# Side work one slot later: VectorE's additions to PE's results, and in_proj's input loaded two blocks ahead

## The chip, the cores and the metric

The kernel runs on one core of a Trainium2 chip. The metric is the device time of one execution in microseconds (us); lower is better. Engines are named as in the profile: PE (TensorE), DVE (VectorE), ACT (ScalarE), POOL (GpSimd) and SP (SyncE, which here issues every DMA). [...]

## The reference

Four layers on a tensor of 4 images x 64 x 64 tokens x 96 channels, all in float32:

```python
x = x + L0(group_norm(x))            # selective scan block, 192 inner channels, on 64 x 64 tokens
x = x + irfft2(L1(rfft2(x)))         # the same kind of block, 384 inner channels, on 64 x 33 frequencies
t = tokens(x)
for layer in (2, 3):
    t = t + attention(layer_norm(t)) # linear attention: (q k^T) v without a softmax, 6 heads
    t = t + ffn(layer_norm(t))       # 96 -> 384 -> 96, operands rounded to 8-bit floats
```

A selective scan block (L0 and L1) does this:

```python
xin, z = split(x @ in_proj_w.T)
u = silu(depthwise_conv3x3(xin) + conv_b)
for k in range(4):                   # rows, columns, and both backwards
    dt, B, C = split(x_proj[k] @ u_k)
    delta = softplus(dt_projs[k] @ dt + bias)
    h_t = h_(t-1) * exp(delta_t * A) + delta_t * u_t * B_t     # 16 states for each channel
    y_k = sum over the states of h_t * C_t
y = layer_norm(sum of y_k + D * u) * silu(z)
return y @ out_proj_w.T
```

## The kernel before

The recurrence is the body of the kernel. Channels lie on the 128 partitions, in three chunks `c`, and tokens on the free axis, in segments of up to 512. There are six **phases**: two for L0 (two images each, 64 partitions per image) and four for L1 (one image each). A phase runs the four directions `k`, each cut into segments; L0 has 8 segments of 512 in a direction, L1 has 5, of 512, 512, 384, 384 and 320. A segment is cut into 12 **steps** (4 groups `q` of four states by 3 chunks `c`). That makes 2 x 384 + 4 x 240 = 1728 steps.

A step has four scan instructions on DVE (L643), two into `hx` and two into `hy`. POOL multiplies `hx` by C (`hcx`, L789) and makes the input of the `hy` scans (L636). DVE multiplies `hy` by C (`hcy`, L807). ACT makes the decays exp(delta A) (L618). PE transposes the input of the next step's `hx` scans (L613) and adds up `hcx` and `hcy` in PSUM (L665). The order on the engines is written out by hand in `scans`; no scheduler moves anything.

Everything else is **side work**: generators that issue a little and then `yield`. In each step the function `slot` is called three times: on DVE's list slot 1 lies after the two `hx` scans, slot 2 between the two `hy` scans, and slot 3, the late one, ahead of `hcy`. On PE's list slot 1 lies ahead of the two transpositions for the next step, slot 2 behind them, and slot 3 between the additions of `hcx` and of `hcy`. A slot adds a third of the phase's entry in `RATES` to a balance and resumes the side work once if the balance is at least one:

```python
prepare_more(kind)
due = min(due + st.z.ph.rate / 3, 3.0)
if due >= 1.0:
    due -= E.step(kind)
```

`E.step` first issues what the generator left with `E.defer` at its last turn, then resumes the generator up to its next `yield`. After `yield LATE` the generator is resumed in a slot 3 only; a refused slot costs no balance. All side work that uses PSUM shares one buffer of one bank (tag `ms`). What a phase has not finished is carried into the next; what is left after the last step is run off with no scans beside it (`E.finish`).

The side work of the phases (with Python's function names) is: `flip0`, `begin0(1)` and two `gate0`; `end0(0)`, `begin1(0)`, `begin1(1)`; `end0(1)`, `begin1(2)`, `begin1(3)`; then `end1(0)`, `end1(1)`, `end1(2)`, one in each of the last three phases. `begin0` for the first two images runs ahead of all phases (the head, up to about 224 us), and `end1(3)` behind them (the tail, from about 11650 us); in both, a `yield` only hands the turn on.

These places of the side work matter here:

- `visits` is in_proj: it loads a block of up to 8 rows of its input (`xi`, L189, 240 to 384 KB, issued on SP), and per block has two turns with PE matmuls (L176). Two buffers (tag `xin`) hold the input; at the beginning of a block the next one is loaded. 48 calls, 228 blocks in all.
- `gated` normalizes: matmuls with the matrix of means into `pm` (L414, three turns), then three DVE subtractions of `pm` from `yb` (L417).
- `out0`: out_proj of L0, two turns of 12 matmuls into `po` (L884), then one DVE addition (L893) and the store of its result.
- `tokens`, attention: four matmuls into `pao` (L1155), then a deferred DVE addition to the tokens (L1157), then the next group's transpositions (L1149).
- `tokens`, feed-forward: matmuls `pfo` (L1184), a deferred ACT copy to `y16` (L1192), then, after `yield LATE`, two DVE additions (L1194, L1198) and the next group's transpositions (L1164).

Of the kernel before, what the change touches and what calls it, by code (L numbers as in the profile page):

```python
# [6 lines left out]
F32 = mybir.dt.float32  # L7
# [10 lines left out]
NB, HH, WW, CH = 4, 64, 64, 96  # L18
# [4 lines left out]
SM = 512  # L23
LATE, BURST = "late", "burst"

RATES = [1.75, 2.25, 2.35, 2.35, 2.35, 2.35]
EXP_LN = "natural_log_exp_and_others"


# [94 lines left out]
class Block:  # L124
# [59 lines left out]
    def visits(self, E, sp, wi, xf, blocks, half, nm, w, done):  # L184


        def load(r, n):
            x = sp.tile([CH, 2, 512], F32, name=f"xi{half}_{nm}_{r}", tag=f"xin{w}", bufs=2)
            self.nc.sync.dma_start(out=x[:, :, : n * 64], in_=xf[:, :, r * 64 : (r + n) * 64])  # L189
            return x  # L190

        nxt = load(*blocks[0])
        yield
        yield
        for b, (r, n) in enumerate(blocks):
            x, nxt = nxt, load(*blocks[b + 1]) if b + 1 < len(blocks) else None
            pi = E.psum(f"pi{half}_{nm}_{r}")
            yield from self.in_proj(pi, wi, half, x, n * 64)
            E.defer(lambda r=r, n=n, pi=pi: done(r, n, pi))
            yield  # L200
# [149 lines left out]
    def gated(self, E, g, io, out_proj):  # L350


        nc, cfg = self.nc, self.cfg
        yn, yo = io["y"][cfg.nat], io["y"][1 - cfg.nat].rearrange("k (w r) c -> r w k c", r=cfg.NR)
        u, gz = io["u"][cfg.nat], io["gz"]
        with E.pool(f"{cfg.pre}nm{g}") as sp:
            wo = sp.tile([P, C, self.w["wo"].shape[2]], F32, name=f"{cfg.pre}_wo_{g}", tag="wo")
            nc.sync.dma_start(out=wo, in_=self.w["wo"])

            tiles = [  # L360
                (b, i, r + i, min(2, n - i)) for b, (r, n) in enumerate(cfg.rows) for i in range(0, n, 2)
            ]

            def load(b, i, r, n):
                nm = f"{cfg.pre}_{g}_{r}"
                yt = sp.tile([P, 2, 2, C * P], F32, name=f"yt_{nm}", tag="yt", bufs=2)
                nc.sync.dma_start(
                    out=yt[: n * 64, 0], in_=yn[:, r * 64 : (r + n) * 64, :].rearrange("k t c -> t k c")
                )
                for m in range(n):  # L370
                    nc.sync.dma_start(out=yt[m * 64 : (m + 1) * 64, 1], in_=yo[r + m])
                ut = sp.tile([P, C, P], F32, name=f"ut_{nm}", tag="ut", bufs=2)
                nc.sync.dma_start(out=ut[:, :, : n * 64], in_=u[:, :, r * 64 : (r + n) * 64])
                return yt, ut

            todo = iter(tiles)
            nxt = load(*next(todo))
            yield
            yield
            yield  # L380
            for b, (r, nr) in enumerate(cfg.rows):
                n = nr * 64
                nm = f"{cfg.pre}_{g}_{r}"
                z = sp.tile([P, C, 512], F32, name=f"zb_{nm}", tag="zb")
                nc.sync.dma_start(out=z[:, :, :n], in_=gz[:, :, r * 64 : r * 64 + n])
                y = sp.tile([P, C, 512], F32, name=f"yb_{nm}", tag="yb")
                for i in range(0, nr, 2):
                    m = min(2, nr - i) * 64
                    yt, ut = nxt
                    more = next(todo, None)  # L390
                    nxt = load(*more) if more else None
                    ps = E.psum(f"py_{nm}_{i}")[:, : C * P].rearrange("p (c t) -> p c t", c=C)
                    for c in range(C):
                        nc.tensor.matmul(
                            ps[:, c, :m], self.skip[:, c, :], ut[:, c, :m], start=(c == 0), stop=False
                        )
                    yield
                    for c in range(C):
                        for k in range(4):
                            nc.tensor.matmul(  # L400
                                ps[:, c, :m],
                                yt[:m, k // 2, k % 2, c * P : (c + 1) * P],
                                self.ident[:m, :m],
                                start=False,
                                stop=(c == C - 1 and k == 3),
                                is_transpose=True,
                            )
                        if c < C - 1:
                            yield
                    E.defer(lambda i=i, m=m, ps=ps, y=y: nc.scalar.copy(y[:, :, i * 64 : i * 64 + m], ps[:, :, :m]))  # L410
                    yield
                pm = E.psum(f"pm_{nm}")
                for c in range(C):
                    nc.tensor.matmul(pm[:, :n], self.mean_w, y[:, c, :n], start=(c == 0), stop=(c == C - 1))  # L414
                    yield
                for c in range(C):
                    nc.vector.tensor_tensor(y[:, c, :n], y[:, c, :n], pm[:, :n], ALU.subtract)  # L417
                yield
                sq = sp.tile([P, C, 512], F32, name=f"sq_{nm}", tag="sq")
                nc.scalar.activation(sq[:, :, :n], y[:, :, :n], AF.Square)  # L420
                yield
                pv = E.psum(f"pv_{nm}")
                for c in range(C):
                    nc.tensor.matmul(pv[:, :n], self.mean_w, sq[:, c, :n], start=(c == 0), stop=(c == C - 1))
                    yield
                ln = sp.tile([P, 512], F32, name=f"ln_{nm}", tag="ln")
                nc.scalar.activation(ln[:, :n], pv[:, :n], AF.Ln, bias=self.eps)
                nc.scalar.activation(pv[:, :n], ln[:, :n], AF.Exp, scale=-0.5)
                yield
                for c in range(C):  # L430
                    nc.vector.scalar_tensor_tensor(
                        y[:, c, :n], y[:, c, :n], self.lnw[:, c : c + 1], pv[:, :n], ALU.mult, ALU.mult
                    )
                yield LATE
                for c in range(C):
                    nc.vector.scalar_tensor_tensor(
                        y[:, c, :n], y[:, c, :n], self.lnb[:, c : c + 1], z[:, c, :n], ALU.add, ALU.mult
                    )
                yield
                yield from out_proj(E, sp, wo, y, r, nr)  # L440
# [429 lines left out]
def out0(images, ins, x0):  # L870


    def task(E, blk, sp, wo, y, r, nr):
        nc = E.nc
        PI = blk.cfg.PI
        tok = slice(r * 64, (r + nr) * 64)
        for i, b in enumerate(images):
            xr = sp.tile([P, 4, CH], F32, name=f"xr_{b}_{r}", tag="xr", bufs=2)
            nc.sync.dma_start(out=xr, in_=ins["x"][b, tok, :].rearrange("(t p) c -> p t c", p=P))
            po = E.psum(f"po_{b}_{r}")[:, : 4 * CH].rearrange("p (t c) -> p t c", t=4)  # L880
            half = slice(i * PI, (i + 1) * PI)
            for m in range(4):
                for c in range(C):
                    nc.tensor.matmul(  # L884
                        po[:, m, :],
                        y[half, c, m * P : (m + 1) * P],
                        wo[half, c, :],
                        start=(c == 0),
                        stop=(c == C - 1),
                    )  # L890
                if m % 2:
                    yield
            nc.vector.tensor_tensor(xr, xr, po, ALU.add)  # L893
            nc.sync.dma_start(out=x0[b][tok, :].rearrange("(t p) c -> p t c", p=P), in_=xr)

    return task
# [144 lines left out]
def tokens(E, ins, consts, ident, x1, b, out):  # L1041
# [4 lines left out]
    with E.pool(f"tk{b}") as sp:  # L1046
# [4 lines left out]
        x = sp.tile([P, NT, CH], F32, name=f"tok_{b}", tag="tok")  # L1051
# [52 lines left out]
        for ly in (2, 3):  # L1104
            nm = f"{b}_{ly}"
# [40 lines left out]
            for g in range(NT // 4):  # L1146
# [7 lines left out]
                for i in range(4):  # L1154
                    nc.tensor.matmul(po[:, i, :], xt[:, i * P : (i + 1) * P], wo, start=True, stop=True)  # L1155
                xs = x[:, g * 4 : g * 4 + 4, :]
                E.defer(lambda xs=xs, po=po: nc.vector.tensor_tensor(xs, xs, po, ALU.add))  # L1157
                yield

            yield from layer_norm(nm + "f")  # L1160
            for g in range(NT // 4):
# [28 lines left out]
                        )  # L1190
                y16 = sp.tile([P, 4, CH], F16, name=f"y16_{nm}_{g}", tag="y16")
                E.defer(lambda y16=y16, po=po: nc.scalar.copy(y16, po))  # L1192
                yield LATE
                nc.vector.tensor_tensor(  # L1194
                    y16, y16, q["b2"].rearrange("p (o c) -> p o c", o=1).to_broadcast([P, 4, CH]), ALU.add
# [206 lines left out]
```

## Time and profile before

| | |
|---|---|
| runs | 12104.8 us median of 3 (12100.4 to 12110.6) |
| profiled execution | 12108.8 us, of which the span of the trace is 12106.9 |
| busy, share of the span | DVE 87%, PE 78%, ACT 75%, POOL 74% |
| granted PE clock | 0.87 of full speed on average |
| scans run | from about 230 to 11650 us: 1728 steps in 11420 us, 6.6 us each |
| tail | 457 us |
| DMA | 44% of 16 engines' time, 120 GB/s |

The page gives busy time of each engine, the span in 40 slices (each digit is the busy share of a slice in tenths), groups of instructions, and who waited for whom. A line such as "DVE a L1 <- PE b L2: 50.0, 10, 9.0" says that DVE sat idle ahead of line 1, which writes a, until PE had done line 2, which writes b: 50.0 us in total, 10 times, 9.0 us at most. "L636 POOL" is line 636 of the kernel on POOL. The views can be cut to a stretch of time.

### The profile page before, as it was taken

To read this page: it belongs to the slowest core of one execution; us is meant where nothing else is said; L and a number is where in the kernel's file an instruction comes from. 1 tells how busy PE (TensorE), PEld (TensorE's weight loads), DVE (VectorE), ACT (ScalarE), POOL (GpSimd) and SP (SyncE) were. 2 spreads that over 40 slices of the span, in tenths; PEclk is the share of its full clock that TensorE was granted. 3 is DMA by queue.
4 is the path that set the end of the run, shared out by engine and by line. 5 is a ranking of instruction groups with operands and counts; after the bars stand their busy time and mean duration, and the time that the engine had idled before them with its cause. 6 is when DMAs were issued, how large, how long until landed. Compare 5 with 4: busy or idle time off the path is not lost. (4 is left out here: it accounts for less than half of the span.)

```text
span 12106.9 us, 164888 instructions
## 1 busy us (share of the span) xinstructions
PE 9441.0 (78%) x54800; PEld 6783.4 (56%) x54800; DVE 10572.7 (87%) x10183; ACT 9071.5 (75%) x18534; POOL 8900.0 (74%) x7074
## 2 busy tenths in 40 slices
PE   5677777777788778777888888788778877887765
PEld 2455555555666556556665565565556555565544
DVE  6899999999999999998879888988989899899854
ACT  3778888898778888887667777777777677777733
POOL 2888889888778888987668877877667766676630
PEclk8889999989889989998879889888878877898886
DMA  5554444556555445445543443444224422452231
GB/s 142 123 135 115 119 125 112 134 157 158 146 143 117 129 130 128 129 132 154 144 120 112 130 123 116 152 128 115 85 91 145 118 82 88 135 132 89 82 103 36
DMA packets 1270447, 1469.07 MB, mean 121 GB/s; under 512 B 496023, under 2 KB 1033823, under 8 KB 1260119
## 3 DMA queue, kind: packets, MB, share of 16 engines
q1 hardware_dynamic: 1269591, 1458.53, 44.1%
q8 instruction: 431, 7.06, 0.2%
q14 instruction: 425, 3.48, 0.1%
HBM read 1221.74 MB, written 236.50 MB: 120 GB/s over the span
## 5 line engine op out<-in xcount | busy, mean ns | idle before, releaser
L636 POOL TENSOR_TENSOR hy_l<-du_l,bc_l 128x512 f32<-128x512 f32 (+2 forms) x3456 | 3956.4, 1165 | 2266.6 <-DVE hcy_l L807 1206.7
L789 POOL TENSOR_TENSOR hcx_l<-hx_l,bc_l 128x1024 f32<-128x1024 f32 (+2 forms) x1616 | 3524.5, 2181 | 279.6 <-DVE hx_l L643 244.1
L593 ACT ACTIVATE bx_l<-dut_l,bt_l 128x192 f32<-128x192 f32 (+2 forms) x6272 | 2771.7, 498 | 0.1
L665 PE MATMUL acc_l<-ident,hcx_l 128*128 128x128 f32 (+1 forms) x12000 | 1885.7, 306 | 357.1 <-POOL hcx_l L789 353.3
L665 PE MATMUL acc_l<-ident,hcy_l 128*128 128x128 f32 (+1 forms) x11994 | 1850.5, 302 | 381.9 <-DVE hcy_l L807 378.5
L618 ACT ACTIVATE ax_l<-delta_l,l_alog 128x512 f32<-128x512 f32 (+2 forms) x3456 | 2139.3, 667 | 0.0
L665 PEld LDWEIGHTS acc_l<-ident,hcy_l 128*128 128x128 f32 (+1 forms) x11994 | 1550.1, 156 | 945.6 <-DVE hcy_l L807 571.3
L665 PEld LDWEIGHTS acc_l<-ident,hcx_l 128*128 128x128 f32 (+1 forms) x12000 | 1545.3, 157 | 852.5 <-POOL hcx_l L789 615.0
L807 DVE TENSOR_TENSOR hcy_l<-hy_l,bc_l 128x1024 f32<-128x1024 f32 (+2 forms) x1615 | 1950.7, 1208 | 43.0
L643 DVE TENSOR_TENSOR_SCAN hx_l<-ax_l,state_l,b_l 128x512 f32<-128x512 f32 (+2 forms) x1648 | 1786.8, 1125 | 222.8 <-PE b_l L613 142.1
L643 DVE TENSOR_TENSOR_SCAN hy_l<-b_l,state_l,hy_l 128x512 f32<-128x512 f32 (+2 forms) x1648 | 1789.7, 1121 | 143.8 <-ACT b_l L618 122.4
L618 ACT ACTIVATE b_l<-delta_l,l_alog 128x512 f32<-128x512 f32 (+2 forms) x1912 | 1200.4, 628 | 881.4 <-DVE hx_l L643 839.3
L613 PE MATMUL b_l<-ident,bx_l 128*128 128x128 f32 (+1 forms) x6718 | 1184.5, 303 | 408.3 <-DVE hy_l L643 193.5
L618 ACT ACTIVATE ab_l<-delta_l,l_alog 128x512 f32<-128x512 f32 x1321 | 909.3, 688 | 700.3 <-DVE hx_l L643 668.7
L613 PEld LDWEIGHTS b_l<-ident,bx_l 128*128 128x128 f32 (+1 forms) x6718 | 825.8, 152 | 905.8 <-DVE hy_l L643 296.7
L643 DVE TENSOR_TENSOR_SCAN hy_l<-ab_l,state_l,hy_l 128x512 f32<-128x512 f32 x961 | 1177.1, 1260 | 97.0 <-ACT ab_l L618 62.0
L643 DVE TENSOR_TENSOR_SCAN hx_l<-ax_l,state_l,ab_l 128x512 f32<-128x512 f32 x962 | 1177.5, 1265 | 95.6 <-PE ab_l L613 66.3
L613 PE MATMUL ab_l<-ident,bx_l 128*128 128x128 f32 x5288 | 903.3, 306 | 454.2 <-DVE hy_l L643 218.0
L656 POOL COPY state_l<-hx_l 128x2 f32<-128x2 f32 x1344 | 1114.3, 829 | 0.0
L613 PEld LDWEIGHTS ab_l<-ident,bx_l 128*128 128x128 f32 x5288 | 653.5, 154 | 799.4 <-DVE hy_l L643 298.5
L272 PE MATMUL pc_l<-pad_l,l_dg 128*128 128x512 f32 (+2 forms) x1656 | 796.5, 569 | 77.9 <-ACT uh_l L250 72.2
L176 PE MATMUL pi_l<-xi_l,l_wi 96*128 96x384 f32 (+6 forms) x912 | 469.0, 629 | 248.2 <-DMA xi_l<-xn 94.8
(193 smaller groups left out, 11970.2 us busy)
## 6 DMA issues: line engine op xcount, KB each, us to landing
bc_l<-l_xd_l SPq DMA_DIRECT2D x1536, 256.0 KB
bc_l<-l_xd_l SPq DMA_DIRECT2D x384, 512.0 KB
bc_l<-l_xd_l SPq DMA_DIRECT2D x384, 384.0 KB
us_l<-l_u SPq DMA_DIRECT2D x96, 768.0 KB
l_y<-y_l SPq DMA_DIRECT2D x288, 256.0 KB
bc_l<-l_xd_l SPq DMA_DIRECT2D x192, 320.0 KB
yt_l<-l_y SPq DMA_DIRECT2D x264, 192.0 KB
yt_l<-l_y SPq DMA_DIRECT2D x128, 384.0 KB
```

Of the source, the lines that this page charges most:

```text
L176: self.nc.tensor.matmul(out[i * cfg.PI : (i + 1) * cfg.PI, :n], wi[:, ki, half, :], xin[:, max(i, ki), :n], start=(ki == 0), stop=(ki == c ...
L272: nc.tensor.matmul(pc[:, : n * 64].rearrange("p (r w) -> p r w", w=64), diag[:, t, :], pad[:, r - p0 + dy : r - p0 + dy + n, dx : dx + 64] ...
L593: nc.scalar.activation(t[:n, b, :, ch], z.dut[:n, b, :, ch], AF.Copy, scale=z.bt[:n, b, m : m + 1])
L613: nc.tensor.transpose(pb[:, t : t + n], st.z.bx[st.q, j][:n, b, st.c], ident[:n, :n])
L618: nc.scalar.activation(out, z.delta[:, st.c, : z.S], AF.Exp, scale=z.blk.A[:, st.c, z.k, n : n + 1])
L636: nc.gpsimd.tensor_tensor(st.hy[:, j, :S], st.z.du[:, st.c, :S], st.z.b[st.q][:, j, :S], ALU.mult)
L643: nc.vector.tensor_tensor_scan(h[:, j, : z.S][:, ::step], a[:, : z.S][:, ::step], b[:, : z.S][:, ::step], 0.0 if z.first else z.state[st.c ...
L656: copy(z.state[st.c][:, n0 : n0 + 2].rearrange("p (j o) -> p j o", o=1), h[:, :, e : e + 1])
L665: nc.tensor.matmul(z.acc[st.c][:n, b, :], hc[:, j, t : t + n], ident, start=(n0 + j == 0 and b == 0), stop=(n0 + j == NST - 1 and b == 0), ...
L789: nc.gpsimd.tensor_tensor(hcx[:, :, :S], hx[:, :, :S], z.c[q][0][:, :, :S], ALU.mult)
L807: nc.vector.tensor_tensor(hcy[:, :, :S], st.hy[:, :, :S], z.c[q][1][:, :, :S], ALU.mult)
```

## The change

Six places change. In `visits` the input has three buffers instead of two; two blocks are loaded at the beginning, and block b + 2 when block b begins; ahead of the first block there are three empty turns instead of two. At L417, L893, L1157 and between L1192 and L1194 one empty `yield` is added, so that what follows it is issued one turn later. The rates of phases 2 to 6 go from 2.25 and 2.35 turns per step to 2.35 and 2.5.

```diff
-RATES = [1.75, 2.25, 2.35, 2.35, 2.35, 2.35]
+RATES = [1.75, 2.35, 2.5, 2.5, 2.5, 2.5]
...
-            x = sp.tile([CH, 2, 512], F32, name=f"xi{half}_{nm}_{r}", tag=f"xin{w}", bufs=2)
+            x = sp.tile([CH, 2, 512], F32, name=f"xi{half}_{nm}_{r}", tag=f"xin{w}", bufs=3)
...
-        nxt = load(*blocks[0])
+        ahead = [load(*blk) for blk in blocks[:2]]
+        yield
         yield
         yield
         for b, (r, n) in enumerate(blocks):
-            x, nxt = nxt, load(*blocks[b + 1]) if b + 1 < len(blocks) else None
+            ahead += [load(*blk) for blk in blocks[b + 2 : b + 3]]
+            x = ahead.pop(0)
...
                 for c in range(C):
                     nc.tensor.matmul(pm[:, :n], self.mean_w, y[:, c, :n], start=(c == 0), stop=(c == C - 1))
                     yield
+                yield
                 for c in range(C):
                     nc.vector.tensor_tensor(y[:, c, :n], y[:, c, :n], pm[:, :n], ALU.subtract)
...
                 if m % 2:
                     yield
+            yield
             nc.vector.tensor_tensor(xr, xr, po, ALU.add)
...
                 xs = x[:, g * 4 : g * 4 + 4, :]
+                yield
                 E.defer(lambda xs=xs, po=po: nc.vector.tensor_tensor(xs, xs, po, ALU.add))
                 yield
...
                 E.defer(lambda y16=y16, po=po: nc.scalar.copy(y16, po))
+                yield
                 yield LATE
                 nc.vector.tensor_tensor(
                     y16, y16, q["b2"].rearrange("p (o c) -> p o c", o=1).to_broadcast([P, 4, CH]), ALU.add
```

## The prediction

> **What bounds the kernel.** First the page (busy shares, slices), then the windows view of the stretch with scans (us; busy us and instructions of PE, PEld, DVE, ACT, POOL; granted clock; DMA).
>
> ```profile
> PE 9441.0 (78%) x54800; PEld 6783.4 (56%) x54800; DVE 10572.7 (87%) x10183; ACT 9071.5 (75%) x18534; POOL 8900.0 (74%) x7074
> ...
> DVE  6899999999999999998879888988989899899854
> ...
> PEclk8889999989889989998879889888878877898886
> ```
> ```profile
> 230.00:11650.00 11420.00, 9030.37 (x52842) 6528.23 (x52842) 10306.02 (x9770) 8878.93 (x18110) 8884.15 (x7041) 0.88 0.45 123
> ```
>
> DVE is at nine tenths nearly throughout: 10306 of 11420 us, 1114 idle. A step lasts 6.6 us, of which its four scans and `hcy` are about 6 at 512 tokens. So DVE sets the pace, and an idle DVE microsecond is a candidate for a gain. The waits of DVE in that stretch say what ends its idle time:
>
> ```profile
> DVE hx_l L643 <- PE b_l L613: 166.8, 97, 7.6
> DVE hy_l L643 <- ACT b_l L618: 141.9, 143, 3.9
> ...
> DVE xr L893 <- PE po L884: 91.6, 28, 9.9
> ...
> DVE tok L1157 <- PE pao L1155: 44.2, 27, 3.7
> DVE yb_l L417 <- PE pm_l L414: 31.5, 20, 4.4
> DVE y L1194 <- ACT y L1192: 31.1, 26, 3.7
> ```
>
> The last four are the places of the change: 91.6 + 44.2 + 31.5 + 31.1 = 198 us in 101 waits, 18% of DVE's idle time. (L417 has 128.0 us more in the tail, where a yield only hands the turn on.) The waits of PE and of SP in the same stretch:
>
> ```profile
> PE pi_l L176 <- DMA xi_l<-xn: 49.6, 8, 8.0
> PE pi_l L176 <- DMA xi_l<-xf: 49.6, 19, 7.4
> ```
> ```profile
> SPq L189 <- PE pi_l L176: 281.1, 74, 9.9
> ```
>
> PE stands 99 us before in_proj for its input. The SP line says why: a load goes out only when PE has left the block before, which frees the buffer. From there it has one block, two turns, or some 4.4 us. The chain of waits, cut to 6800 to 7900 us, has 4.3% (47 us) in such loads, the pieces 4.7 to 9.6 us long: more than 4.4.
>
> Last the timeline around the longest wait of L893, and the window over it:
>
> ```profile
> 3052.06 2.87 PE L884 MATMUL po<-l_wo,yb_l 64*128 64x96 f32 x12
> ...
> 3054.86 1.97 PE L613 MATMUL b_l<-ident,bx_l 128*128 128x128 f32 x8
> ...
> 3056.76 2.87 PE L884 MATMUL po<-l_wo,yb_l 64*128 64x96 f32 x12
> ...
> 3059.67 0.56 DVE L893 TENSOR_TENSOR xr<-xr,po 128x384 f32<-128x384 f32 x1 [9.90 <-PE po L884]
> 3060.14 1.22 DVE L807 TENSOR_TENSOR hcy_l<-hy_l,bc_l 128x1024 f32<-128x1024 f32 x1
> ```
> ```profile
> 3050.00:3060.00 10.00, 10.00 (x43) 8.78 (x42) 0.33 (x1) 1.74 (x4) 0.00 (x0) 0.50 0.08 21
> ```
>
> PE is busy throughout at half clock (0.50), and DVE stands although `hcy` and the next two `hx` scans, whose transpositions ended at 3056.8, need nothing from `po`. Only the order on DVE holds them.
>
> [...] twelve matmuls of L884 take 2.87 us here and 1.57 us at 2945.6[...] PE stayed at 0.50 while fully busy from 3040 to 3060. Cutting the stretch at each change of clock gives 2808 us at half clock, DVE 83.0% busy, and 8612 at full, DVE 92.6% busy.
>
> **The change, part by part.** No instruction is added or removed; the same 228 loads are issued.
>
> *Turns.* Counted from the loops: 42 more in `visits`, 31 in `gated`, 32 in `out0`, 48 each in attention and feed-forward, 201 in all, on 3398 used before. Walking `slot` with the old rates ends the side work in step 1722 of 1728, and the trace agrees (last L1194 with scans: step 1721). With the new turns and rates it ends in step 1726, and each `require` finds its work done; so nothing runs off uncovered. With the old rates 115 turns would be left over, at about 1.0 us each (209 turns of `tokens` take 214 us in the tail). This edit costs nothing, its cover being the 5184 slots.
>
> *Additions.* Each wait shrinks by what DVE does in one slot: 1.2 us (one `hy` scan) for an addition in slot 1 or 2, 3.7 us (`hcy` and two `hx`) in slot 3. By place on DVE's timeline, with each wait cut at that: L893 58.6 of 91.6 (17 of 28 in slot 3), L1157 37.4, L417 27.6, L1194 31.1 (all in slot 3; the copy now goes out in slot 2). Sum 155 us. Not all reaches the end: after the wait another input may be late, first the transpositions (L613 already holds `hx` for 167 us) and POOL's L636. Bounds 0.3 (PE is the limit at half clock) and 1; I take 0.7, since at full clock DVE is 93% busy: **108 us**.
> What moves along: the store of `xr` behind L893 (0.37 us on SP), ACT's squares behind L417, PE's transpositions behind L1157 and L1194. Each stands right behind its addition as before, so none gains a wait. POOL's side work changes its step only.
>
> *Loads.* The load of b + 2 waits for the same event, PE leaving block b − 1, so nothing waits longer behind it on SP; it has two blocks, 8.8 us, instead of one. Of 99 us some 88 go; waits over 4.4 us keep a rest. At each of 42 visits with scans a second load, 0.6 us on SP, goes out ahead of the broadcasts behind it; SP is mostly waiting anyway, so nothing is taken. PE isn't the pace maker: at 7501.3 PE waited 4.15 us while DVE ran on. Bounds 0 and 99; I take half: **44 us**. In the head, 37 of 45 us of these waits are for the normalized input itself; I take 0, bounds −5 to +5.
>
> *Tighter pace.* Filled slots go from 78% to 83% of the chances, and side work that hands from PE to ACT and back over the single `ms` bank has fewer gaps to recover in. These PE waits (L394, L272, L176, L1172, L1155, L414, L968) sum to 371 us; 6% more is 22, of which 0.6 reach DVE: 14 us lost. Bounds 0 and 40.
>
> Sum: −108 − 44 + 14 = −138. Profiled execution 12108.8 → 11971; the median stands 4.0 below it, so **11967**.
>
> **Rivals.**
> *The waits only change rows.* DVE arrives at the next scan earlier and stands for PE or ACT there. For: PE at half clock for a quarter of the time, and 286 us of `hx` waits on PE. Against: the free work in the timeline above. At a share of 0.1: −15 − 10 + 14, about 12094, no change.
> *More than the sum.* [...] a microsecond moved from half to full clock is worth (0.926 − 0.830) / 0.926 = 0.10 us. All 155 + 99 and 400 us less at half clock: −254 − 41 + 14, about 11824.
> *The wait turns round, slower.* All these tiles lie in one bank, so the next group's transpositions (L1149) or the next image's matmuls (L884) can't start before DVE has read. Now PE comes first and stands for the late addition, with the next step's transpositions behind it, and DVE meets that at its next scan. For: the single bank[...]. Against: today PE waits there for 0.2 to 1.1 us, 6 us in all, and in each slot it waits for DVE's scans anyway. Place: 80 additions (32 L893, 48 L1157). A full slot of 2.2 us each is 176 us, against 138: 12143. It decides from 1.7 us per addition.
> *The change doesn't do what it says:* the count of turns rules that out, as long as the third buffer (4 KB per partition) fits.
>
> **How the numbers follow.** Forecast 62%; more than the sum 8%; rows only 13%; turned round 17%. From no change a measurement of this kernel can tell about 0.2%, 24 us. Faster: 62 + 8 + 4 of the rows case = 0.74; same 0.08; slower 17 + 1 = 0.18. The range goes from 11865 (155 + 85 at full share) to 12130, which takes in the rows case and the mild end of the reversal; about 1 in 10 is left on either side.
>
> **What would show it.** Right: in the stretch with scans L893 + L1157 + L417 + L1194 fall from 198 to some 50 us, L1194 to nearly none; PE's waits for `xi` from 99 to under 20; DVE's idle time to about 980; busy times and the tail (457 us) unchanged. Wrong: `hx` waits on L613 up by as much as the additions lost; or PE waits at L1149 and L884 for DVE above 100 us; or side work left after the last scan.

## The result and the profile after

The kernel after takes **11952.4 us** (median of 4 runs, 11944.9 to 11959.3) against 12102.6 for the kernel before: a ratio of 0.9876, with a 95% interval of 0.9858 to 0.9893, or 150 us less. Forecast were 11967 and 138 us less. The profiled execution took 11954.5 us. Lines have moved: the scans are now L646, `hcy` L810, and the four places of the change L420 (before L417), L897 (L893), L1162 (L1157) and L1200 (L1194).

Busy time and clock on the page after, and the windows view of its stretch with scans, which now ends at 11492 us:

```profile
PE 9389.2 (79%) x54800; PEld 6740.0 (56%) x54800; DVE 10568.1 (88%) x10183; ACT 9071.9 (76%) x18533; POOL 8891.4 (74%) x7075
...
PEclk9889999888898898898889889898889888898786
```
```profile
224.00:11492.00 11268.00, 8977.34 (x52839) 6482.52 (x52836) 10300.86 (x9770) 8879.61 (x18108) 8874.92 (x7042) 0.88 0.45 125
```

DVE does the same 10.3 ms of work as before. Its idle time in the stretch is 11268 − 10301 = 967 us, where it was 1114. That is the gain: 147 us of the 152 by which the stretch is shorter. DVE's waits there:

```profile
DVE hy_l L646 <- ACT b_l L621: 179.7, 157, 9.2
DVE hx_l L646 <- PE b_l L616: 161.7, 115, 9.4
...
DVE y L1200 <- ACT y L1197: 26.4, 31, 1.6
...
DVE xr L897 <- PE po L887: 16.2, 9, 3.8
...
DVE tok L1162 <- PE pao L1159: 8.1, 11, 1.7
```

With 0.6 us at L420 the four places have 51 us left of 198, 147 less; so DVE's other waits, taken together, stayed the same. `xr` fell most, from 91.6 to 16.2. The line of `hx` behind PE's transpositions didn't swell (before 166.8), so the time that was won wasn't handed to that wait. The line of `hy` behind ACT did swell, from 141.9 to 179.7; about 20 of these 38 us come with the new rates alone (162.3 in `e6_rates_only` below). PE's and SP's waits for in_proj's input:

```profile
PE pi_l L176 <- DMA xi_l<-xf: 19.1, 7, 4.6
PE pi_l L176 <- DMA xi_l<-xn: 13.6, 2, 8.7
```
```profile
SPq L189 <- PE pi_l L176: 234.1, 59, 12.6
```

PE waits 33 us for it instead of 99. SP still stands behind the same event, PE leaving a block; only what it then fetches is wanted later.

To see where along the run the gain arises, take the start of the `hcy` of step n, counted from that of step 0. The columns are before, after, and the difference to before added in that stretch:

| to step | side work in the stretch (after) | before | after | added |
|---|---|---|---|---|
| 384 | flip0, begin0, gate0 (only `visits` has changed) | 2634 | 2589 | −44 |
| 506 | end0(0) | 3514 | 3438 | −31 |
| 770 | begin1(0), begin1(1) | 5281 | 5233 | +28 |
| 885 | end0(1) | 6054 | 5954 | −52 |
| 1137 | begin1(2), begin1(3) | 7589 | 7472 | −18 |
| 1727 | end1(0), end1(1), end1(2) | 11422 | 11269 | −36 |

One row goes the wrong way: in the first pair of `begin1` time is lost. The experiments say to what.

### The profile page after: what moved, and what is told of

Its sections match the earlier page's. It is cut to its first block, busy times and chain, and to the rows that moved or that the text cites. A ratio compares the mean times of both kernels' runs of the same rounds, so it can differ in the third digit from the quotient of the medians.

```text
span 11952.7 us, 164822 instructions
## 1 busy us (share of the span) xinstructions
PE 9389.2 (79%) x54800; PEld 6740.0 (56%) x54800; DVE 10568.1 (88%) x10183; ACT 9071.9 (76%) x18533; POOL 8891.4 (74%) x7075
## 5 line engine op out<-in xcount | busy, mean ns | idle before, releaser
L810 DVE TENSOR_TENSOR hcy_l<-hy_l,bc_l 128x1024 f32<-128x1024 f32 (+2 forms) x1616 | 1947.9, 1205 | 43.5
L646 DVE TENSOR_TENSOR_SCAN hx_l<-ax_l,state_l,b_l 128x512 f32<-128x512 f32 (+2 forms) x1650 | 1787.8, 1124 | 202.0 <-PE b_l L616 134.8
L646 DVE TENSOR_TENSOR_SCAN hy_l<-b_l,state_l,hy_l 128x512 f32<-128x512 f32 (+2 forms) x1649 | 1789.6, 1120 | 158.5 <-ACT b_l L621 147.5
L646 DVE TENSOR_TENSOR_SCAN hy_l<-ab_l,state_l,hy_l 128x512 f32<-128x512 f32 x961 | 1175.8, 1258 | 86.2 <-ACT ab_l L621 53.6
L646 DVE TENSOR_TENSOR_SCAN hx_l<-ax_l,state_l,ab_l 128x512 f32<-128x512 f32 x962 | 1176.5, 1264 | 55.9 <-PE ab_l L616 35.7
```

The lines of the kernel that those rows point to most:

```text
L646: nc.vector.tensor_tensor_scan(h[:, j, : z.S][:, ::step], a[:, : z.S][:, ::step], b[:, : z.S][:, ::step], 0.0 if z.first else z.state[st.c ...
L810: nc.vector.tensor_tensor(hcy[:, :, :S], st.hy[:, :, :S], z.c[q][1][:, :, :S], ALU.mult)
```

## The experiments

Each time stands beside runs of the kernel before on the same chip; differences in us are the ratio less one, times 12100.

**The two parts by themselves.** `e1_loads_only` is the kernel before with the loads alone, turns and rates as before. `e2_adds_only` has the four turns ahead of the additions and the new rates, with the old `visits`.

```diff
 # e1_loads_only, on the kernel before
-... tag=f"xin{w}", bufs=2)
+... tag=f"xin{w}", bufs=3)
-        nxt = load(*blocks[0])
+        ahead = [load(*blk) for blk in blocks[:2]]
...
-            x, nxt = nxt, load(*blocks[b + 1]) if b + 1 < len(blocks) else None
+            ahead += [load(*blk) for blk in blocks[b + 2 : b + 3]]
+            x = ahead.pop(0)
```

> The kernel before with three input buffers in visits and block b + 2 loaded at block b, and nothing else: turns and rates as before. Theory (two separate gains that add up): in the first phase, where the change touches only visits, step 384 came 44 us earlier after than before, so this run gains at least those 44 us, and some 15 to 25 more in the begin1 stages: 12035 to 12060, PE's waits for xi from 99 us to 30 to 40. Rival (the additions are the whole gain, PE's waits for xi lie beside DVE's work): 12090 to 12105.

> The kernel before with the four empty turns ahead of the additions and the new rates; visits as before (two buffers, one block ahead, two turns). Theory: the four places fall from 198 us of DVE waits to about 50 as in the kernel after, and 0.7 of the 148 reach the end: 11990 to 12015, the four places at 45 to 60 us. With the run of the loads alone the gains add up to about 150. Rival (the waits only change rows): within 25 us of 12103, with the waits of hx on L613 up by 100 us. Rival (the loads were the whole gain): the same time.

Measured: the loads 12049.3 us, ratio 0.9955 (0.9943 to 0.9968), −54 us; the additions 12059.2 us, ratio 0.9964 (0.9950 to 0.9977), −44 us. So both are worth something, and neither rival that gives all to one part holds. The loads came by less in the first phase than expected (18 us at step 384, not 44), and PE's waits for `xi` fell to 53 us, not to 30 to 40. The additions gained at most half of the 88 to 113 us that were expected, although their waits in the trace fell nearly as expected:

```profile
DVE xr L895 <- PE po L885: 30.4, 13, 4.8
...
DVE y L1198 <- ACT y L1195: 26.5, 34, 1.9
...
DVE tok L1160 <- PE pao L1157: 8.1, 10, 1.6
...
DVE yb_l L418 <- PE pm_l L414: 3.2, 5, 1.4
```

These sum to 68 us, 130 less than before, but DVE's idle time fell only from 1114 to 1035. Ahead of the scans DVE now waits longer, in the rows of `b_l`, `ab_l` and `_l` (one name, which the profile cuts at its front) together: at `hx` for PE 325 us instead of 291, and at `hy` for ACT 280 instead of 248. Something in the same kernel takes back a part of what the additions give.

**The same turns at another place, and the rates alone.** `e3_turns_behind` has the same number of turns and the same rates as `e2_adds_only`, but each turn stands behind its addition. `e6_rates_only` is the kernel before with the new rates and nothing else. `e4_old_rates` is the kernel after with the old rates.

```diff
 # e3_turns_behind, on the kernel before (L893's; the other three likewise), with the new RATES
             nc.vector.tensor_tensor(xr, xr, po, ALU.add)
             nc.sync.dma_start(out=x0[b][tok, :].rearrange("(t p) c -> p t c", p=P), in_=xr)
+            yield
```
```diff
 # e6_rates_only, on the kernel before; e4_old_rates is the reverse on the kernel after
-RATES = [1.75, 2.25, 2.35, 2.35, 2.35, 2.35]
+RATES = [1.75, 2.35, 2.5, 2.5, 2.5, 2.5]
```

> The same number of empty turns and the new rates as in the run of the additions alone, but each empty turn stands behind the addition instead of ahead of it (behind L417's three, behind L893's store, behind L1157's deferral, behind L1198). Theory (it is the distance from matmul to addition that pays): the four places stay at 150 to 200 us of DVE waits and the time is 12080 to 12125. Rival (it is the thinner side work or another lie of the turns against the steps): a gain like that of the turns ahead, 11990 to 12015.

> The kernel before with the new rates and no new turns: the side work is 4 to 6% denser and runs out earlier, in step 753 of 768 and 1677 of 1728. Theory (denser side work costs more than in proportion, which is where the 60 to 75 us of the run with the turns behind went): the busy stretches lose more than the empty steps win back, 12120 to 12170. Rival (the cost is in proportion, and those 75 us came from the place of the turns): 12090 to 12115.

> The kernel after with the old rates 2.25 and 2.35. By the count of turns 115 are left over after the last step and run with no scans beside them. Theory (the rates only keep the side work covered; an uncovered turn costs about 1.0 us, less what the thinner side work saves in the steps): the last scan comes 0 to 60 us earlier than the 11486 us of the kernel after, the tail grows from 467 by 90 to 130 us, and the time is 12000 to 12060. Rival (rates don't matter, the side work ends with the scans anyway): 11940 to 11965. Rival (the tighter pace costs more than the uncovered turns): below 11940.

Measured: turns behind 12177.6 us, ratio 1.0062 (1.0050 to 1.0075), **+75 us**; rates alone 12140.4 us, ratio 1.0037 (1.0025 to 1.0050), **+45 us**; old rates 12042.1 us, ratio 0.9948 (0.9936 to 0.9961), −63 us, so some 90 us slower than the kernel after. DVE's waits with the turns behind:

```profile
DVE xr L894 <- PE po L885: 80.9, 25, 8.2
...
DVE tok L1159 <- PE pao L1157: 51.5, 35, 4.0
...
DVE yb_l L417 <- PE pm_l L414: 22.0, 16, 3.7
...
DVE y L1197 <- ACT y L1195: 22.0, 27, 3.6
```

The four places are back at 176 us, and the time lies above the 12080 to 12125 that was expected. `e3_turns_behind` and `e2_adds_only` ran on the same chip and differ only in where the turns stand; between them lie 118 us (12177.6 − 12059.2). But the four places, 176 against 68 us, are not all that differs. In `e3_turns_behind` DVE also waits at a fifth place, in the feed-forward, for the ACT copy of PE's `ph` to `h`; the turn behind L1198, the only new one there, fits as what moves this work nearer to its matmul. First `e2_adds_only`, then `e3_turns_behind`:

```profile
DVE h L1179 <- ACT h L1176: 6.3, 9, 1.1
```
```profile
DVE h L1179 <- ACT h L1176: 47.5, 48, 3.5
```

Before, this wait was 9.7 us. From the end of the `ph` matmul to this DVE work it is now 1.6 us (median of 48) instead of 2.7. So the two kernels differ by 149 us of waits for distance (108 + 41), and 118 us of them reached the time: a share of 0.8. The windows view agrees. First `e3_turns_behind`, then `e2_adds_only`:

```profile
224.00:11705.00 11481.00, 9029.11 (x52870) 6545.98 (x52868) 10323.93 (x9775) 8886.09 (x18121) 8880.68 (x7045) 0.88 0.45 122
```
```profile
224.00:11577.00 11353.00, 8976.86 (x52877) 6486.60 (x52875) 10318.46 (x9777) 8887.09 (x18127) 8883.76 (x7046) 0.88 0.45 124
```

DVE's idle time falls by 123 us, from 1157 to 1035; the rest, 25 us, came back ahead of the scans. A second comparison needs no turns behind: `e6_rates_only` has the rates of `e2_adds_only` and no new turns, and its four places have 201 us. Against it `e2_adds_only` has 133 us less of these waits and is 88 us faster by the ratios (107 us if the 19 us are added that `e6_rates_only` wins where its side work has run out): a share of 0.7 to 0.8. So it is the distance from matmul to addition that pays, at 0.7 to 0.8 us for each microsecond of wait, uncertain by some 0.15 from the intervals of the runs.

The pace costs. `e6_rates_only` does the same work as the kernel before and is 45 us slower, although its last 51 steps have no side work and win 19 us (from step 1530 on). So a denser side work costs more than in proportion. DVE's idle time there is 1143 us instead of 1114, spread over several rows (`hy` behind ACT's `b_l` 162 us instead of 142, `hx` behind POOL's `hy` 28 instead of 12); which mechanism makes them longer isn't shown. That `e3_turns_behind` is 30 us slower still fits the 40 us more at `h` and the side work in its last 51 steps; it is no sign that an empty turn costs by itself.

In `e4_old_rates` the last `hcy` (the range of starts in the row of L810) comes earlier than after, and the tail is longer. First the kernel after, then `e4_old_rates`:

```profile
L810 DVE TENSOR_TENSOR hcy_l<-hy_l,bc_l x1616: 806/1225/2357, 217.1 to 11486.1; 128x1024 f32<-128x1024 f32 x128, 128x768 f32<-128x768 f32 x35, 128x640 f32<-128x640 f32 x17
```
```profile
L810 DVE TENSOR_TENSOR hcy_l<-hy_l,bc_l x1624: 809/1225/2160, 217.0 to 11434.2; 128x1024 f32<-128x1024 f32 x128, 128x768 f32<-128x768 f32 x35, 128x640 f32<-128x640 f32 x18
```

The steps win 52 us, and the tail grows from 467 to 604 us, by 137 (90 to 130 were expected): 1.2 us for each of the 115 turns that are left over. So the rates had to go up with the turns.

**What in `visits` pays.** `e5_turn_only` adds the third empty turn at the beginning of a visit to the kernel before, and nothing else but rates of 2.29 and 2.38 to hold it. `e7_loads_and_turn` has all of the change to `visits`, at the same rates.

> The kernel before with one more empty turn at the beginning of each visit (three instead of two), two buffers and one block ahead as before; phases 2 and 3 at rates 2.29 and 2.38, which just hold the 42 more turns. In the first phase (rate the same in all kernels) step 384 came 18 us earlier with the loads alone and 44 us earlier with loads and turn. Theory (the turn lets the first block land, by itself): step 384 comes 15 to 30 us earlier than before, and the time is 12070 to 12100. Rival (the turn helps only where a second load is queued behind the first): step 384 within 8 us of before, time 12100 to 12130.

> The kernel before with all of the change to visits (three buffers, two blocks ahead, three turns) and none of the additions; rates 2.29 and 2.38 in phases 2 and 3. Theory: step 384 comes 44 us earlier as in the kernel after, PE's waits for xi are 30 to 35 us, and the time is 12010 to 12040, so that this and the run of the additions alone account for 110 to 145 of the 150 us. Rival (the two parts need each other): 12040 to 12060, no better than the loads alone.

Measured: the turn 12054.3 us, ratio 0.9967 (0.9954 to 0.9979), −40 us; both 12030.0 us, ratio 0.9947 (0.9934 to 0.9959), −64 us. Step 384 came 18 us earlier with the loads, 41 with the turn, 42 with both, 44 in the kernel after. So in the first phase the turn alone does nearly as much as both together, and more than the 15 to 30 us that were expected of it. The waits in that phase, with the loads alone and then with the turn alone (before: 32.3 at `hx`, 49.6 for `xi`):

```profile
DVE hx_l L644 <- PE b_l L614: 25.3, 10, 10.1
...
PE pi_l L176 <- DMA xi_l<-xn: 19.0, 3, 8.7
```
```profile
DVE hx_l L644 <- PE b_l L614: 15.3, 6, 8.6
...
PE pi_l L176 <- DMA xi_l<-xn: 14.3, 2, 8.8
```

Both bring PE's wait for the input down, the turn a little further, and the turn halves DVE's wait behind PE. That wait fits as the way by which a late load reaches the end: PE stands, its transpositions come late, DVE's scan waits. With the rows of `ab_l` it is 53 us before, 40 with the loads and 22 with the turn, 13 and 31 us less, in step with the 18 and 41 us gained; PE's own wait fell by 31 and 35. The turn also spreads the phase's side work over more steps at the same rate (the last in_proj matmul of the phase comes in step 384 instead of 376); how much of its gain is that was not separated. Outside the first phase the loads add to the turn: −64 against −40, a difference only just outside the two intervals together. Over the whole run the two parts overlap: the loads alone gave 54 us, the turn alone 40, both 64. PE's waits for `xi` with both were 43 us, not the 30 to 35 expected.

**Does the sum close?** `e2_adds_only` and `e7_loads_and_turn` make −108 us together, the kernel after −150. `e9_adds_fit` is `e2_adds_only` with rates of 2.30 and 2.45 in phases 2 and 3, and `e12_after_again` the kernel after once more on the same chip.

> The additions alone once more, with rates that just hold their 159 turns: 2.30 and 2.45 in phases 2 and 3 (side work ends in steps 768, 1132, 1720) instead of 2.35 and 2.5 (764, 1126, 1714). The gains of the additions alone (44 us) and of visits alone (63 us) were 42 us short of the whole. Theory (the run of the additions alone paid for a pace that it didn't need): 12020 to 12045 against 12103, 20 to 35 us less than that run, and the sum closes to within 25 us. Rival (the parts help each other beyond their sum): 12050 to 12065.

> The kernel after, unchanged, beside the others on the same chip. Every theory: a ratio of 0.986 to 0.989 to the kernel before.

Measured: 12058.6 us, ratio 0.9968 (0.9957 to 0.9980), −39 us; and 11965.2 us, ratio 0.9888 (0.9875 to 0.9902), −136 us. The additions alone did not pay for a needless pace: that theory fell. Between the sum of the parts and the whole 28 to 47 us are missing, depending on the pair of runs; three intervals of about 15 us each make some 26 us together, if they are independent. So the sum does not quite close. Whether the parts help each other stays open.

**The turn ahead of L1200.** `e10_no_ffn_turn` is the kernel after without the `yield` between the copy to `y16` and `yield LATE`.

> The kernel after without the empty turn between the copy to y16 and the LATE turn of its additions (48 turns fewer with scans; the side work still ends in step 1725, since a refused slot takes the place). After, DVE still waited 26 us there, of 31 before. Theory (that turn bought next to nothing, PE's pfo being late itself): within 15 us of the kernel after. Rival (the turn is worth its 31 us of waits): 20 to 35 us above the kernel after.

Measured: 11991.4 us, ratio 0.9915 (0.9901 to 0.9928), 26 us more than `e12_after_again` on the same chip. So the turn earns its place, against my theory. DVE's wait there was 40.5 us without it; of the other half of the 26 us no row tells.

**Other loads.** `e8_ut_ahead` loads `ut` in `gated` two tiles ahead in three buffers. `e11_first_loads` is the kernel after with two more turns at the beginning of `gated`, one in `fourier` and in `inverse`, and the feed-forward weights issued ahead of the others with one more turn; rates 2.36, 2.52 and 2.53.

```diff
 # e11_first_loads, on the kernel after (gated's part)
             nxt = load(*next(todo))
             yield
             yield
             yield
+            yield
+            yield
```

> The kernel after with the same idea in gated: the input ut of the skip matmuls (L396) in three buffers and loaded two tiles ahead, yt as before. After, PE waits 29 us for ut with scans running, six times, and more in the tail. Theory (a wait of PE for a load reaches the end at 0.5 to 0.9): 11920 to 11940, PE's waits for ut near none with scans. Rival (these six waits lie beside DVE's work, or the loads queue behind others on SP all the same): 11945 to 11960.

> The kernel after with more time for first loads: two more empty turns at the beginning of gated, one each for fourier and inverse, the feed-forward weights w1 and w2 loaded ahead of the other weights and one more turn before they are used; rates 2.36, 2.52 and 2.53 to hold the 23 more turns. After, these waits were 29 us (ut), 27 (weights), 13 (at), 6 (xw) with scans. Theory (as in visits, what is left are first loads, and each microsecond of them reaches the end at about 0.8): 11895 to 11925 against the kernel after at 11952, the four rows together under 25 us. Rival (the tighter pace takes it back): 11940 to 11965.

Measured: `ut` ahead 11947.8 us, ratio 0.9885 (0.9870 to 0.9901), the same as the kernel after. More time for first loads: **11931.5 us**, ratio 0.9863 (0.9850 to 0.9877), the fastest kernel here, 34 us below `e12_after_again` beside it. PE's wait for `ut` after, and with `ut` two tiles ahead:

```profile
PE py_l L396 <- DMA ut_l<-l_u: 28.9, 6, 8.4
```
```profile
PE py_l L402 <- DMA ut_l<-l_u: 27.1, 5, 8.1
```

It hardly moved. Five waits are left, and the trace has them at the first matmul of each of the five runs of `gated` with scans (steps 388, 773, 1140, 1337 and 1533): what is late is the first tile of each, which no loading ahead can help. In the tail, where the later tiles were late too, loading ahead did help: these waits fell from 32 to 10 us, and the tail from 467 to 459. With more turns for first loads the same rows, and the wait for the weights (before it 26.6 us) and at `y16`:

```profile
PE py_l L398 <- DMA ut_l<-l_u: 23.1, 8, 5.3
```
```profile
DVE y L1211 <- ACT y L1208: 14.4, 24, 1.5
...
DVE qw L1136 <- DMA w<-in_l_w: 8.0, 3, 4.9
```

Of these rows the weights and, unasked, `y16` fell most, by 19 and 13 us; which of them gave the 34 us was not separated. At the first tiles of `gated` two more turns left 19 of 28 us. The rows of first loads together went from 76 us (`e12_after_again`) to about 47, not to the 25 that I expected, and the time stayed just above the 11895 to 11925 expected.

## Why the prediction was right, and where it was off

The direction, the size (−138 against −150, and −136 in `e12_after_again`) and the way of it were right: DVE's idle time fell to 967 us where "about 980" was forecast, with busy times unchanged. That the size fits so well is in part luck. Two terms of the sum were too small, with opposite signs, and the two changes measured apart leave 28 to 47 us of the whole without an account:

| term | forecast | measured |
|---|---|---|
| additions | −108 | −88 (`e2_adds_only` against `e6_rates_only`) to −118 (against `e3_turns_behind`, which also lost at `h`) |
| tighter pace | +14, at most 40 | +45 (`e6_rates_only`, 30 to 60) |
| `visits` | −44 | −64 (`e7_loads_and_turn`) |

- *Additions.* Cutting each wait at what DVE does in one slot gave 155 us; the waits fell by 147. The share of 0.7 for what reaches the end held: 0.7 to 0.8 in the runs. The reason for its lower bound, 0.3 where PE is the limit at half clock, did not show: of the 147 us of idle time that went, 103 lay in stretches at half clock (476 to 373 us) and 44 at full (638 to 594). In `e12_after_again`, the same kernel, it was 72 and 62. That the four places came to 51 us where "some 50" was forecast hides two misses. The cut left 33 us at `xr`, and 16 were measured; it left nothing at `y16`, and 26 were measured.
- *L1194.* "To nearly none" was wrong: 26.4 of 31.1 us stayed. The copy does go out in slot 2, but it is late itself. The timeline after:

```profile
8565.88 1.14 PE L1189 MATMUL pfo<-qw,h 128*128 128x96 fp8e5 x12
...
8567.05 0.48 ACT L1197 CAST y<-pfo 128x384 f16<-128x384 f32 x1 [0.97 <-PE pfo L1189]
...
8567.56 0.56 DVE L1200 TENSOR_TENSOR y<-y,b 128x384 f16<-128x384 f16 x1 [1.44 <-ACT y L1197]
```

  PE's `pfo` ends 0.03 us ahead of the copy, and the copy ends as the addition starts. I had moved the copy and not asked what it waits for. The turn is still worth its place, by some 26 us (`e10_no_ffn_turn`).
- *Loads.* I gave the whole term to the second block of lead, and counted the third empty turn at nothing beyond its slot. By itself that turn is worth 40 us, and the loads by themselves 54; together they are worth 64, so that the turn is no small addition and the two can't be split. I had also read two turns as 4.4 us, which holds only for turns in neighbouring slots: in the trace before, the blocks of in_proj start 8.4 us apart in the first phase and 6.1 after it (medians). PE's waits for `xi` fell to 33 us, not under 20; 8.7 us of that is a single wait in the first phase.
- *Pace.* The term took 6% more of 371 us of PE's waits for ACT, 22 us. The runs give about three times the 14 us, near or above the upper bound of 40, and not by that way: in `e6_rates_only` the same waits are 379 us, 8 more, and in the kernel after 340. What carries the rest isn't shown. In the kernel after it shows as the row of +28 us in `begin1`, which got denser side work and no addition of the four: in the same steps, 506 to 770, `e6_rates_only` loses 20 us, and `e2_adds_only` and `e3_turns_behind`, at the same rate, 35 and 36.
- *Rivals.* The wait that turns round did not come: after, PE waits 5.5 us at L1153 and 1.8 us at L887 for DVE's additions, far from the 1.7 us for each of 80 that it needed. "Rows only" did not come either: the `hx` waits on PE, in the rows of `b_l` and `ab_l`, went down, from 286 to 262 us. With the additions alone they grew by 34 us (with `_l`, 291 to 325), and with the change to `visits` alone they fell by 52 (to 239). The clock may have helped a little: 2669 us at half clock instead of 2808, which at the prediction's 0.10 us each is an estimated 14 us; that wasn't separated from the rest, and what moved the clock was not shown. The count of turns held: the side work ended with the scans, and the tail is 467 us (before 461).

## What to carry to other kernels

Where the engine that sets the pace takes hand-placed side work in the order of its list, as DVE did here before (9.90 us at L893 with free work behind it), put one slot of its own work between a producer's last instruction and its consumer; here each microsecond of such a wait was worth 0.7 to 0.8 of a microsecond. Price the pace at which the rest then has to run by itself: here it cost 45 us beside a gain of 150. When such a gain is checked with the turns at another place, look for the waits that the other place makes. And look at what waits remain after loading ahead: if there is one for each call, at its first use, it is the first load, and a longer start is what is left to try; here it took 9 of 28 us.

## What the runs showed of the hardware

PE's waits for `xi` fell from 99 to 33 us, but the share of time at half PE clock (0.50 granted) hardly changed. It was 24.6% of the stretch before (2808 of 11420 us) and 23.7% after (2669 of 11268), in 385 and 373 separate pieces. So here a PE that stood 66 us less for DMA spent 139 us less of 2808 at half clock. That the one brought the other was not shown; a gain through the clock, as in the second rival, was my estimate.
